# Packing in pieces, moments by tile, and response tables partly on GpSimd, in a Macaron block with 4-bit weights

## The chip, the cores and the metric

The kernel runs on one core of one Trainium2 chip. The metric is the device time of one execution in microseconds. Lower is better. The engines are TensorE (PE; its weight loads are PEld), VectorE (DVE), ScalarE (ACT) and GpSimd (POOL); SyncE (SP) issues nearly all of the transfers.

## The reference

The input is `u`, 2 x 1024 rows of 1024 values, in float32. Three layers with a residual follow each other:

```python
x = u
x = x + 0.5 * ffn(layernorm(x))
x = x + s4(layernorm(x))
x = x + 0.5 * ffn(layernorm(x))

# ffn: 4-bit weights, 8 to a 32-bit word; a scale and a zero point for each group of 128 rows
W = (nibble - (zero + 1)) * scale            # Wg, Wu: 1024 x 2752;  Wd: 2752 x 1024
out = (silu(x @ Wg) * (x @ Wu)) @ Wd

# s4: a causal convolution along the 1024 values of each row
K = s4_kernel(Lambda, p, q, Vc @ Bp, Ct, exp(log_step), 1024)   # needs 1024 complex roots and an inverse DFT
y = irfft(rfft(x, 2048) * rfft(K, 2048))[:1024] + D * x
```

The convolution kernel `K` depends on the parameters alone, and is computed once in the kernel.

## The kernel before

The 2048 rows are four blocks of 512 (`TB`). A block passes twice through the feed-forward layer, which makes eight jobs, in the order of `JOBS`; the convolution of a block lies in the gate/up stage of the job that follows its first pass.

**A job has two stages.** `gate_up` runs over 64 steps: eight waves (`WAVES`) of two or three column tiles of gate and up, and in each wave the eight groups of 128 input rows. The block is held transposed as a high and a low part (`xTh`, `xTl`), so each weight tile is multiplied twice (line 628). The scale of a group is brought in by rescaling: after each group but the last, the accumulator in PSUM is multiplied by the ratio of two groups' scales, on ScalarE for the gate units and on VectorE for most of the up units (`scaled`, lines 598 and 600). After the last group, `gated` makes the product with SiLU (`hf`) and splits it into `hh` and `hl` (lines 655 to 662). `down` runs over 44 steps: two halves of 512 columns, and 22 tiles of the inner dimension in each, with four accumulators that are rescaled in the same way after each of the first 20 tiles. In job 0, ScalarE also takes the second of the four at every other step. `back` turns a finished half and adds it to `x`.

**Weights.** In job 0 the 4-bit words become bytes that are written to device memory (`wq`, `wdq`); every job then loads bytes four steps ahead (`load_bytes`) and converts them three steps ahead to full values (`make_weights`), mostly on GpSimd, in five buffers. Making the bytes has four parts. `fetch` and `fetch_zeros` (for the down matrix `fetch_down`) load words and zero points through SP. `split` and `take_zeros` (`split_down`) run six operations on VectorE: two shifts with masks (lines 453 and 454), and for the even and the odd half an add of the zero points and an xor (lines 461 and 462). `dequantize` (`dequantize_down`) copies each of the eight nibble positions to a byte tile (lines 478 and 510), mostly on GpSimd, and writes it out. The work of wave `w` stands around step `8 * w - 12`, and that of the six row tiles of the down matrix from step 52 of gate/up to step 29 of down.

**Other work.** `moments` and `deviations` compute mean and inverse deviation for 512 rows on VectorE (`BN_STATS` at line 182, then a Newton iteration); `normalized` and `turn` make the transposed block of the next job. In job 1, the tables of the convolution are made by the generator `s4_tables`: poles and weights (`s4_poles`), sums over them by TensorE and the algebra of the roots (`s4_roots`), the response (`s4_response`: `s_k`, line 915) and its Toeplitz blocks `near`, `after`, `ahead`, `middle` (`s4_toeplitz`). Before the change all elementwise work of these but four operations and two fills is on VectorE. One step of the generator is taken in each of 40 steps of gate/up.

**What sets the order.** `fast` hangs functions into dictionaries of hooks by step (`at`), and the stage calls them when it reaches the step. A scheduler then sets the final order of each engine's queue from the dependences. Only what is written through `in_order_of_writing` is held, on the engines named, behind the last instruction of that engine written before it. Two lines show both forms:

```python
at(up, s0 - 1, lambda both=both: in_order_of_writing(both, ET.DVE))   # packing of a wave: held on VectorE
at(up, s, lambda: next(tables, None))                                  # a piece of the tables: not held
```

## Time and profile before

| What | Value |
|---|---|
| median of 3 runs | 2164.68 us (2164.53 to 2165.5) |
| the profiled execution's own time | 2165.84 us |
| its span | 2164.1 us |
| mean granted TensorE clock | 0.993 |
| PE, DVE, ACT, POOL busy | 97%, 80%, 66%, 48% |
| job 0: gate/up, down | 29.1 to 202.8 us, 202.4 to 310.9 us |
| job 1: gate/up, down | 310.9 to 519.8 us, 519.4 to 605.6 us |
| a later job without convolution (7): gate/up, down | 1912.4 to 2069.9 us, 2069.6 to 2151.3 us |

The span is counted from the first to the last instruction; the time holds what lies around it too. The stages in the table are those of the first and last matmuls of their kind. A matmul's record can include some waiting, so a window is judged by its length beside that of the same steps in another job, and the busy time is a hint. A line number is that of the kernel before; in the profile of the changed kernel the same statement has a higher number.

### The profile page before, as it was taken

The numbers are of one execution on the slowest core, as the hardware profiler recorded it, in microseconds if no ns is written. First come the engines' busy times: TensorE is split into PE (matmuls) and PEld (weight loads), VectorE is DVE, ScalarE is ACT, GpSimd is POOL, SyncE is SP. The second block draws the span as 40 slices with busy tenths as digits, with TensorE's granted clock in tenths as the row PEclk, the third lists the DMA queues.
The fourth block names the chain that finished last, engine by engine and source line by source line (L and its number), as shares of the span: only waits on it lengthen the run. The fifth ranks groups of instructions, "written<-read, shape, count | busy, mean of one in ns | idle before, by whom it ended". The sixth has DMA issues, their size and how long they took to land.

```text
span 2164.1 us, 30241 instructions
## 1 busy us (share of the span) xinstructions
PE 2097.0 (97%) x9748; PEld 1429.4 (66%) x9748; DVE 1723.0 (80%) x2831; ACT 1422.9 (66%) x2233; POOL 1038.7 (48%) x1366
## 2 busy tenths in 40 slices
PE   5999899899999999999999999999999999999998
PEld 3555676476867568665776558676686766866576
DVE  7889787778887877778777787878778787777776
ACT  5887677546754677676667767646776467767765
POOL 3868835444345453455335553445534455345642
PEclk9999999999999999999999999999999999999999
DMA  4433321112111311211321121112111121121111
GB/s 141 122 95 116 113 65 42 43 46 80 37 39 51 97 45 46 80 34 33 111 76 42 31 72 35 41 52 74 37 34 40 54 93 44 47 81 36 33 35 57
DMA packets 163543, 132.48 MB, mean 61 GB/s; under 512 B 22252, under 2 KB 151029, under 8 KB 163376
## 3 DMA queue, kind: packets, MB, share of 16 engines
q1 hardware_dynamic: 162528, 129.12, 19.7%
q8 instruction: 79, 1.29, 0.3%
q10 hardware_dynamic: 592, 1.25, 0.2%
q14 instruction: 88, 0.72, 0.1%
q0 software_dynamic: 256, 0.10, 0.0%
HBM read 104.79 MB, written 25.50 MB: 60 GB/s over the span
## 4 chain that ended last, share of the span: by engine, by line
PE 86%; DVE 8%; DMA 2%; POOL 2%; issue 1%; ACT 0%; SPq 0%; DVEq 0%; POOLq 0%; ACTq 0%
PE pg L628 52%; PE po L691 27%; PE pc L993 3%; DVE pg L600 2%; PE pb L713 1%; PE pb L993 1%; DVE po L600 1%; PE pt L219 1%; PE st L219 1%; DVE hf L658 1%; POOL qd L510 1%; DMA raw<-in_L_ffn_up_qweight_dram 0%; PE s_k L915 0%; ACT g L655 0%; DVE hb L674 0%
## 5 line engine op out<-in xcount | busy, mean ns | idle before, releaser
L598 ACT ACTIVATE pg<-pg,rat 128x512 f32<-128x512 f32 x1240 | 786.5, 660 | 435.7 <-PE pg L628 435.0
L600 DVE TENSOR_TENSOR pg<-pg,rat 128x512 f32<-128x512 f32 x1168 | 776.2, 693 | 168.3 <-PE pg L628 163.5
L628 PE MATMUL pg<-xTh,w_up 128*128 128x512 f32 x2752 | 855.1, 438 | 8.3 <-DVE pg L600 6.0
L628 PE MATMUL pg<-xTl,w_up 128*128 128x512 f16 x2752 | 722.8, 383 | 12.4 <-DVE w_up L572 6.6
L576 POOL CAST w_up<-b 128x768 fp32r<-128x768 int8 (+2 forms) x487 | 375.2, 775 | 566.6 <-PE pg L628 454.9
L628 PEld LDWEIGHTS pg<-xTh,w_up 128*128 128x128 f32 x2752 | 519.7, 189 | 185.1 <-DVE pg L600 23.3
L691 PE MATMUL po<-hl,w_down 128*128 128x512 f32 x1344 | 542.7, 406 | 15.5 <-DVE po L600 11.4
L598 ACT ACTIVATE po<-po,ratd 128x512 f32<-128x512 f32 x660 | 431.9, 662 | 167.7 <-PE po L691 167.3
L691 PE MATMUL po<-hh,w_down 128*128 128x512 f32 x1344 | 525.9, 393 | 0.0
L600 DVE TENSOR_TENSOR po<-po,ratd 128x512 f32<-128x512 f32 x620 | 427.1, 697 | 94.1 <-PE po L691 89.9
L628 PEld LDWEIGHTS <-w_up 128*128 128x128 bf16 x2752 | 228.6, 99 | 336.5 <-issue 152.5
L576 POOL CAST w_down<-bd 128x512 fp32r<-128x512 int8 x352 | 222.6, 634 | 417.8 <-PE po L691 357.8
L691 PEld LDWEIGHTS po<-hl,w_down 128*128 128x128 f32 x1344 | 253.9, 189 | 91.9 <-DVE po L600 24.3
L691 PEld LDWEIGHTS po<-hh,w_down 128*128 128x128 f32 x1344 | 254.7, 190 | 45.8
L662 POOL TENSOR_TENSOR hl<-hf,hh 128x512 fp32r<-128x512 f32 x168 | 217.4, 1294 | 8.4
L658 DVE SCALAR_TENSOR_TENSOR hf<-pg,rat,g 128x512 f32<-128x512 f32 x168 | 123.2, 748 | 45.0 <-ACT g L655 39.9
L655 ACT ACTIVATE g<-pg,rat 128x512 f32<-128x512 f32 x168 | 110.8, 687 | 51.2 <-PE pg L628 41.1
L660 POOL CAST hh<-hf 128x512 fp32r<-128x512 f32 x168 | 106.2, 632 | 63.3 <-PE pg L628 37.1
L182 DVE BATCH_NORM_STATS2 stats<-x 128x6 f32<-128x512 f32 x96 | 63.3, 675 | 0.4
L1023 DVE TENSOR_TENSOR x<-x,pc 128x512 f32<-128x512 f32 x32 | 22.0, 686 | 36.4 <-PE pc L993 36.4
L219 PE MATMUL pt<-ident,xn 128*128 128x128 f32 x256 | 43.8, 288 | 7.3 <-ACT xn L1371 7.3
L242 DVE TENSOR_TENSOR xTl<-pt,xTh 128x512 f16<-128x512 f32 x56 | 38.3, 688 | 13.7 <-ACT xTh L241 12.9
(177 smaller groups left out, 1047.8 us busy)
## 6 DMA issues: line engine op xcount, KB each, us to landing
b<-wq SPq DMA_DIRECT2D x319, 96.0 KB
bd<-wdq SPq DMA_DIRECT2D x336, 64.0 KB
x<-in_L_attn_u_dram SPq DMA_DIRECT2D x30, 512.0 KB
b<-wq SPq DMA_DIRECT2D x128, 64.0 KB
xs<-x SPq DMA_DIRECT2D x16, 512.0 KB
x<-xs SPq DMA_DIRECT2D x16, 512.0 KB
out_dram<-x SPq DMA_DIRECT2D x16, 512.0 KB
b<-wq SPq DMA_DIRECT2D x64, 80.0 KB
```

The source lines that it names most:

```text
L182: nc.vector.bn_stats(stats[:, t, i, :], x[b][t][:, bass.ts(i, 512)])
L219: nc.tensor.transpose(ps[:, bass.ts(k, P)], n[:, bass.ts(k, P)], ident)
L576: nc.gpsimd.tensor_copy(t, b)
L598: nc.scalar.activation(dst, src, AF.Copy, scale=sc)
L600: nc.vector.tensor_tensor(dst, src, sc.to_broadcast([P, TB]), ALU.mult)
L628: nc.tensor.matmul(p, weights, (lo, hi)[k][:, g, :], start=(g == 0 and not done), stop=(g == GK - 1 and done), skip_group_check=True,)
L655: nc.scalar.activation(g, pg, AF.Silu, scale=rat[:, 2 * f, GK - 1 :])
L658: nc.vector.scalar_tensor_tensor(hf, pu, last, g, ALU.mult, ALU.mult)
L660: nc.gpsimd.tensor_copy(hi, hf)
L662: nc.gpsimd.tensor_tensor(lo, hf, hi.bitcast(F32), ALU.subtract)
L691: nc.tensor.matmul(ps[c], w[:, bass.ts(c, P)], part, start=(f == 0 and k == 0), stop=(f == NF - 1), skip_group_check=True,)
L993: nc.tensor.matmul(dst, lhsT, rhs, start=start, stop=stop, skip_group_check=True)
```

## The change

Four things are changed, and no arithmetic of the result.

1. `split`, `take_zeros` and `split_down` become one generator, `signed_bytes`, with six pieces. `in_pieces` hangs each piece at a step of its own and holds it in the order of writing on VectorE. The loads for a wave are issued five steps ahead instead of three, those for a row tile of the down matrix seven units ahead instead of three.
2. `moments` becomes a generator by row tile; in job 0 its five pieces lie in steps 3 to 7 of the down stage instead of all in step 0, and what follows from them six steps later than before.
3. The tables of the convolution are cut into 63 pieces over 42 steps, held on VectorE. About half of the elementwise work goes to GpSimd, the large operations in halves of 512 columns.
4. In job 1 the convolution and what follows stand four steps later. In job 0 the block is loaded again at step 27 of the down stage instead of 21, with the turns back at steps 32 to 41; in the other jobs these turns come one step earlier.

The core of the diff:

```diff
     def moments(b, k, then=None):
+        for _ in moments_by_tile(b, k, then):
+            pass
+
+    def moments_by_tile(b, k, then=None):
...
             if then:
                 then(t, mv[:, t, 0:1])
+            yield
...
-    def bytes_of(raw, even):
+    def signed_bytes(key, raw, even, z):
         nc.vector.tensor_scalar(even, raw, 3, NIBBLES, ALU.logical_shift_left, ALU.bitwise_and)
+        yield
         nc.vector.tensor_scalar(raw, raw, 1, NIBBLES, ALU.logical_shift_right, ALU.bitwise_and)
-        return even, raw
-    def signed(part, z):
-        both = part.bitcast(U16)
-        nc.vector.tensor_tensor(both, both, z.bitcast(U16), ALU.add)
-        nc.vector.tensor_scalar(both, both, 0x8080, None, ALU.bitwise_xor)
-        return part.bitcast(I8).rearrange("p (n k) -> p k n", k=4)
+        yield
+        for part in (even, raw):
+            both = part.bitcast(U16)
+            nc.vector.tensor_tensor(both, both, z.bitcast(U16), ALU.add)
+            yield
+            nc.vector.tensor_scalar(both, both, 0x8080, None, ALU.bitwise_xor)
+            yield
+        view = lambda a: a.bitcast(I8).rearrange("p (n k) -> p k n", k=4)
+        packed[key] = view(even), view(raw)
...
+    def in_pieces(at, hooks_and_steps, pieces):
+        held = {}
+        def piece(last):
+            def step():
+                if not held:
+                    held[0] = pieces()
+                for _ in held[0]:
+                    if not last:
+                        break
+            in_order_of_writing(step, ET.DVE)
+        for i, (hooks, s) in enumerate(hooks_and_steps):
+            last = i == len(hooks_and_steps) - 1
+            at(hooks, s, lambda last=last: piece(last))
...
-                at(up, s0 - 3, lambda both=both: in_order_of_writing(both, ET.SP))
-                both = lambda w=w: (split(w), take_zeros(w))
-                at(up, s0 - 1, lambda both=both: in_order_of_writing(both, ET.DVE))
+                at(up, max(0, s0 - 5), lambda both=both: in_order_of_writing(both, ET.SP))
+                steps = [(up, max(1, s0 - d)) for d in (3, 2, 2, 1, 1, 1)]
+                in_pieces(at, steps, lambda w=w: split(w))
...
-                at(*when(max(0, n - 3)), lambda a=a, rt=rt: fetch_down(a, rt))
-                at(*when(max(0, n - 1)), lambda a=a, rt=rt: split_down(a, rt))
+                at(*when(max(0, n - 7)), lambda a=a, rt=rt: fetch_down(a, rt))
+                steps = [when(max(0, n - d)) for d in (4, 3, 3, 2, 1, 0)]
+                in_pieces(at, steps, lambda a=a, rt=rt: split_down(a, rt))
...
-        nc.vector.scalar_tensor_tensor(di, cs, neg[:, 1:2], di, ALU.mult, ALU.add)
+        for own in halves:
+            yield
+            nc.vector.scalar_tensor_tensor(
+                di[:, own], cs[:, own], neg[:, 1:2], di[:, own], ALU.mult, ALU.add
+            )
...
-        nc.vector.tensor_tensor(den, dr, dr, ALU.mult)
...
-        nc.vector.tensor_tensor(sq, di, di, ALU.mult)
-        yield
-        nc.vector.tensor_tensor(den, den, sq, ALU.add)
+        for own in halves:
+            yield
+            nc.gpsimd.tensor_tensor(den[:, own], dr[:, own], dr[:, own], ALU.mult)
+            yield
+            nc.gpsimd.tensor_tensor(sq[:, own], di[:, own], di[:, own], ALU.mult)
+            yield
+            nc.gpsimd.tensor_tensor(den[:, own], den[:, own], sq[:, own], ALU.add)
         for c in range(NC):
             yield
             nc.vector.reciprocal(den[:, bass.ts(c, P)], den[:, bass.ts(c, P)])
...
-        nc.vector.tensor_tensor(poles[0:NST], dr[0:NST], den[0:NST], ALU.mult)
-        yield
-        nc.vector.tensor_tensor(poles[NST:P], di[NST:P], den[NST:P], ALU.mult)
+        for own in halves:
+            yield
+            nc.gpsimd.tensor_tensor(poles[0:NST, own], dr[0:NST, own], den[0:NST, own], ALU.mult)
+            yield
+            nc.gpsimd.tensor_tensor(poles[NST:P, own], di[NST:P, own], den[NST:P, own], ALU.mult)
...
         def op(o, l, r, f):
...
-            nc.vector.tensor_tensor(tmp[o], l, r, f)
+            nc.gpsimd.tensor_tensor(tmp[o], l, r, f)
...
-            nc.vector.tensor_tensor(m0, ec, wide(x0), mul)
-            nc.vector.tensor_tensor(m1, es, wide(x1), mul)
-            nc.vector.tensor_tensor(m0, m0, m1, f)
+            nc.gpsimd.tensor_tensor(m0, ec, wide(x0), mul)
+            nc.gpsimd.tensor_tensor(m1, es, wide(x1), mul)
+            nc.gpsimd.tensor_tensor(m0, m0, m1, f)
+            yield
             nc.vector.tensor_reduce(se[:, i, :], m0, AX.X, add)
...
-        nc.vector.tensor_copy(near[:, 0:3], blocks[:, 0:3])
-        nc.vector.tensor_copy(near[:, 3], blocks[:, 4])
+        yield
+        nc.gpsimd.tensor_copy(near[:, 0:3], blocks[:, 0:3])
+        nc.gpsimd.tensor_copy(near[:, 3], blocks[:, 4])
...
-            nc.vector.tensor_tensor(own, blocks[:, d : d + 5 : 2], blocks[:, 2:7:2], ALU.subtract)
+            nc.gpsimd.tensor_tensor(own, blocks[:, d : d + 5 : 2], blocks[:, 2:7:2], ALU.subtract)
...
+    S4_PIECES = 63
...
-                    late = 30 if j == 1 else 0
+                    late = 34 if j == 1 else 0
...
-                for s in range(2, 42):
-                    at(up, s, lambda: next(tables, None))
+                for i in range(S4_PIECES):
+                    piece = lambda: in_order_of_writing(lambda: next(tables, None), ET.DVE)
+                    at(up, 1 + 42 * i // S4_PIECES, piece)
...
-                    stage, o = (dn, 0) if j == 0 else (up, 44)
-                    at(stage, o, lambda: in_order_of_writing(lambda: moments(ab, 1), ET.DVE))
-                    at(stage, o + 1, lambda: deviations(ab, 1, LIFT))
+                    if j == 0:
+                        steps = [(dn, d) for d in range(3, 8)]
+                        in_pieces(at, steps, lambda: moments_by_tile(ab, 1))
+                        newton = lambda: deviations(ab, 1, LIFT)
+                        at(dn, 8, lambda: in_order_of_writing(newton, ET.DVE))
+                    else:
+                        both = lambda: moments(ab, 1)
+                        at(up, 44, lambda: in_order_of_writing(both, ET.DVE))
+                        at(up, 45, lambda: deviations(ab, 1, LIFT))
...
-                o = 3 if j == 0 else 0
+                o = 9 if j == 0 else 0
...
-            at(dn, 21, lambda: load_x(b, rows_of(u, b) if k == 1 else saved(b)))
+            o, gap = (27, 3) if j == 0 else (21, 4)
+            at(dn, o, lambda: load_x(b, rows_of(u, b) if k == 1 else saved(b)))
             for t in range(NT):
-                at(dn, NF + 5 + 4 * t, lambda t=t: back(b, 0, t))
+                at(dn, o + 5 + gap * t, lambda t=t: back(b, 0, t))
```

## The prediction

> **What bounds the kernel now.** I read the page first, then windows by stage, then who waited for whom in the slow stages, then single groups. TensorE holds the end:
>
> ```profile
> span 2164.1 us, 30241 instructions
> PE 2097.0 (97%) x9748; PEld 1429.4 (66%) x9748; DVE 1723.0 (80%) x2831; ACT 1422.9 (66%) x2233; POOL 1038.7 (48%) x1366
> ...
> PE 86%; DVE 8%; DMA 2%; POOL 2%; issue 1%; ACT 0%; SPq 0%; DVEq 0%; POOLq 0%; ACTq 0%
> ```
>
> The 97% says little of where time can come from, as a stage that waits and one that does not are averaged. The windows view sets each stage of jobs 0 and 1 beside the same stage of a later job, which has the same matmuls and none of the one-time work (columns: window, its length, busy us of PE, PEld, DVE, ACT, POOL, clock, DMA share, GB/s):
>
> ```profile
> 29.10:157.00 127.90, 126.11 (x556) 72.97 (x557) 108.48 (x191) 103.26 (x166) 88.96 (x107) 0.99 0.36 104
> 157.00:202.40 45.40, 42.01 (x177) 22.55 (x176) 42.68 (x66) 33.87 (x56) 38.56 (x53) 1.00 0.52 153
> 202.40:263.00 60.60, 51.39 (x207) 36.72 (x206) 51.88 (x83) 37.32 (x61) 48.16 (x63) 0.92 0.30 93
> 263.00:309.60 46.60, 43.51 (x190) 33.92 (x189) 34.23 (x79) 34.93 (x55) 17.12 (x27) 0.96 0.29 81
> 309.60:519.40 209.80, 200.59 (x982) 129.19 (x980) 164.92 (x302) 121.26 (x194) 93.94 (x118) 0.99 0.15 45
> 519.40:564.40 45.00, 43.98 (x206) 34.89 (x205) 36.20 (x54) 31.84 (x51) 17.78 (x26) 1.00 0.25 79
> 564.40:605.60 41.20, 41.20 (x190) 33.61 (x188) 33.54 (x51) 27.78 (x44) 14.46 (x23) 1.00 0.15 43
> 605.60:793.30 187.70, 187.36 (x929) 122.95 (x929) 153.92 (x272) 112.53 (x178) 92.91 (x118) 1.00 0.19 58
> 2029.40:2069.70 40.30, 40.30 (x179) 23.73 (x177) 29.39 (x44) 28.74 (x45) 20.84 (x30) 1.00 0.14 39
> ```
>
> Row 2 (job 0, gate/up steps 44 to 63) against row 9 (the same steps of job 7): 5.1 us over, DVE 94% busy. Row 3 (job 0, down steps 0 to 21) against row 6: 15.6 over. Row 4 (down steps 22 to 43) against row 7: 5.4 over. Row 5 (job 1, gate/up) against row 8 (job 2): 22.1 over. Row 1 is some 10.5 over job 7's 117.3 us (from the starts of the matmuls of those steps), but 7.2 of that is before 60 us, in the start, whose order hardly changes. From 605 us on there is nothing to win. So this change is worth at most what it takes from about 50 us.
>
> What ends the waits in rows 3 and 4, and TensorE's waits in row 5 (us in total, times, longest):
>
> ```profile
> PE po L691 <- DVE po L600: 8.2, 4, 3.5
> ...
> DVE s_vc L807 <- DMA s_vc<-in_L_attn_Bp_dram: 3.6, 1, 3.6
> ...
> DVE rawd L461 <- DMA zd<-zd_dram: 3.3, 1, 3.3
> PE po L691 <- DVE s_vc L760: 3.1, 1, 3.1
> ```
>
> ```profile
> PE pg L628 <- DVE pg L600: 6.7, 3, 3.8
> PE pb L993 <- POOL sums L988: 1.7, 1, 1.7
> PE s_t L951 <- DMA s_rows<-k_dram: 0.5, 1, 0.5
> ```
>
> It is VectorE each time: a matmul may not go on in a bank until VectorE has scaled it (L600), and the scaling stands behind packing, moments or tables in its queue. Twice VectorE itself stands behind a load.
>
> **The change, part by part.** The sum is made against the profiled execution (span 2164.1, time 2165.84 us); the median of the runs, 2164.68, lies 1.2 below its time, so I subtract the gain from the median.
>
> *Packing in gate/up, job 0.* No instruction goes or comes: two shifts, two adds, two xors for each of eight waves and six row tiles, all still on VectorE. Fetches move two steps earlier on SP's queue, past the writes of the bytes (L482) and the loads of weights (L558) there; the wave's pieces start up to two steps earlier, one to three together between scalings, where the old blocks already had scalings between their parts. The buffers' waits are few, as far as the order shows, so I cost the moved issues at nothing; the cover is the load of weights four steps ahead (about 11 us). If it is gone, GpSimd's conversion is late and TensorE waits about a DMA, 2 us. Row 1: gain 1, ends 0 and 3.
>
> Row 2: before, all three packings of the first column half of down lie here; the order of the changed kernel puts the 88-row one behind `hb`, in the down stage. Price of one:
>
> ```profile
> L461 DVE TENSOR_TENSOR rawd<-rawd,zd 88x1024 uint16<-88x1024 uint16 x2 | 2.2, 1104 | 3.3 <-DMA zd<-zd_dram 3.3
> L462 DVE TENSOR_SCALAR rawd<-rawd 88x1024 uint16<-88x1024 uint16 x2 | 2.3, 1128 | 0.0
> ```
>
> with shifts of 0.65 and 0.79: 5.9 us. DVE falls from 42.7 to 36.8 in a stage that can be 40.3 long, so it is no longer its bound. Bunching still costs about 1.3: 41.8, gain 3.6 (ends 1 and 5).
>
> *Down, first half (row 3).* Here the VectorE sum decides, and it gets more work, not less: 51.9 busy, plus the 88-row packing 5.9, minus the two last pieces of the last packing, which now come after the outputs `y` (1.10 + 1.13 = 2.2), plus one `y` scaling that fell outside the window, 0.7: 56.3 us against TensorE's 45.0. Moments by tile (eight BN_STATS of 0.67, four aggregates of 0.20) cost the same 6 us in five pieces. What goes is the 3.3 us wait for `zd`: its fetch is now seven units ahead instead of three, 3.3 steps or 6 us more. Idle of VectorE remains for ScalarE's gate at the start (1.4) and some for TensorE: 58.5. Gain 2.1; ends 56.3 (gain 4.3) and, if all other idle time stays (8.7 - 3.3), 61.7 (loss 1.1). GpSimd's transposed tiles move from steps 5 to 19 to steps 11 to 25 and meet its `qd` copies (0.77 each); 48 busy of 60 before says it still fits while VectorE holds the pace.
>
> *Down, second half (row 4).* The tables no longer start here, being tied to the order of writing in job 1: the 3.6 us wait for `Bp` goes with the wait it caused. Comes: two turned halves (eight cost 45.0 against 40.6 in job 7, so 1.1 for two) and 2.2 of packing, with half of it hidden. 41.2 + 1.1 + 1.0 = 43.3, gain 3.3 (ends 1 and 5). In later jobs the back transposes come one step earlier; the same instructions, cost nothing, covered by the free banks; 0.2 a job if not.
>
> *Tables (row 5).* 11.7 of the 22.1 is TensorE's own work that stays: 7.5 for `s_k` (L915), 1.7 `s_sums`, 2.5 `s_t`. The rest is stalls, 6.7 of them on VectorE. To GpSimd go 3.6 (L786 to L791), 2.8 (poles), about 1.3 of 128x64 products, the 128x8 operations and 6 of Toeplitz blocks. The row that shows what that is worth, VectorE above and GpSimd below at the same time:
>
> ```profile
> 380.29 1.80 DVE L867 TENSOR_TENSOR s_work<-s_work 128x8 f32<-128x8 f32 x3
> ...
> 382.25 3.91 DVE L867 TENSOR_TENSOR s_work<-s_work 128x8 f32<-128x8 f32 x7
> ```
>
> ```profile
> 382.15 1.28 POOL L662 TENSOR_TENSOR hl<-hf,hh 128x512 fp32r<-128x512 f32 x1
> ```
>
> A 128x8 operation takes 0.17 alone; three of them stretch to 1.2 each while GpSimd works on `hl`, and TensorE's longest wait (3.8, at 386.8) follows. On GpSimd they queue behind `hl` without holding scalings.
>
> The rule that speaks against this is the Trainium skill's GPSIMD Engine Reference, section "Engine selection": elementwise work belongs on VectorE, GpSimd being about twice as slow with two inputs. The trace agrees: 1.29 us for 128x512 on GpSimd (L662), 1.22 for 128x1024 on VectorE (L786). By the rule the table chain gets slower: six squares and sums 7.8, four poles 5.2, 28 small at 0.19 (nearest row: the 128x1 copy, L384), six 128x64 about 0.3, Toeplitz 6, in all about 26 us; were it on the path, that would cost 12 more than VectorE's 14. By the trace GpSimd has 94 of 210 us busy here, and 120 still fits. I take the trace's side for the load, and the rule's for latency: VectorE now waits in order for GpSimd at the first reciprocal, at L875, L878 and both L898. Following the order with these durations, GpSimd is one or two steps early at the reciprocals and within about 1 us of need at the last four. New waits: 0 to 8, I take 1. Moments and convolution four steps later (late 34) end nearer to the next turn: 0.5. Net gain 5 (ends -5 and 9).
>
> Sum: 1 + 3.6 + 2.1 + 3.3 + 5 = 15.0; 2164.7 - 15.0 = 2149.7, and I say 2149.5.
>
> **The rivals.** (A) As summed: half of the stalls go; 13 to 20 us, 2145 to 2152.
>
> (B) VectorE stays the bound. For it: row 3 gets work added. Then row 3 gives -1, row 2 about 2, and GpSimd's latency eats most of row 5 (1 to 2): with 1 and 3, a gain of 6 to 7, 2158.
>
> (C) Spreading ends nearly all stalls: row 3 at 56.3, row 2 at 40.5, row 5 at 9, row 4 at 5, row 1 at 2: 4.3 + 4.9 + 9 + 5 + 2 = 25, 2139. Against: 56.3 is already a VectorE without idle time.
>
> (D) Slower, by one mechanism: the table chain's handovers. VectorE's queue is in order, so a wait at L875, L878 or L898 holds the scalings behind it, and TensorE with them. GpSimd's queue holds `hl` (1.3), `hh` (0.6) and conversions (0.85) that themselves wait for TensorE to free a weight buffer (a step, 2.7). If each of the four comes behind two steps of that, 5.4 each, row 5 loses 21.6 and gains 6: against 10 from the rest that is 2170. It decides from about 4 us at each. Against: conversions run three steps ahead, and GpSimd is idle half the time.
>
> (E) The edits only trade places (the stalls of row 5 come back at GpSimd, row 3 is held by VectorE): within 0.2%, that is 4.3 us, about what a measurement of this kernel tells from no change.
>
> **How the numbers follow.** A 0.55, B 0.22, C 0.13, E 0.06, D 0.04. The range leaves out the far part of C below 2138, E above 2160 and D: 2138 to 2160, about 0.83. Faster by over 0.2%: A, B, C, 0.90; within: 0.06; slower: 0.04.
>
> **What would show it.** In the windows of the changed profile: job 0's steps 44 to 63 near 42 us; its down stage near 102 instead of 107, the first half with VectorE over 95% busy and no wait for `zd`; no `s_vc` work before 300 us; job 1's gate/up near 205 instead of 210, with small TENSOR_TENSOR on POOL and the waits of PE on DVE below 3 us. I am wrong in row 3 if VectorE has idle time there while TensorE waits; wrong in row 5 if DVE waits for POOL `s_work` or `s_cos` by several us; and wrong in kind if anything after 620 us differs by over 2 us.

## The result, and the profile after

The changed kernel takes 2152.4 us in the median of 4 runs (2151.76 to 2153.46), the kernel before 2164.98 in the same comparison (2164.53 to 2165.5). The ratio is 0.9942, with a 95% interval of 0.9925 to 0.996: 12.6 us faster. The profiled execution took 2152.6 us, its span is 2150.7. Its page:

```profile
span 2150.7 us, 30258 instructions
PE 2092.5 (97%) x9748; PEld 1425.5 (66%) x9748; DVE 1704.3 (79%) x2783; ACT 1422.3 (66%) x2233; POOL 1062.5 (49%) x1420
```

These lines hardly differ from those of before. The windows view of the changed kernel, cut at the same steps as the nine rows of the prediction (same columns; rows 7 and 8, 41.3 and 187.7 us long, are left out), tells where the time went:

```profile
29.00:164.40 135.40, 127.33 (x555) 73.84 (x556) 113.77 (x192) 103.75 (x166) 92.62 (x107) 0.97 0.34 98
164.40:209.20 44.80, 42.04 (x178) 22.84 (x176) 37.89 (x59) 34.17 (x56) 32.40 (x44) 1.00 0.55 163
209.20:261.70 52.50, 47.34 (x199) 32.57 (x198) 49.18 (x85) 35.69 (x59) 41.22 (x58) 1.00 0.23 66
261.70:305.40 43.70, 42.67 (x197) 34.09 (x195) 29.91 (x45) 33.59 (x55) 28.43 (x42) 1.00 0.42 129
305.40:505.60 200.20, 199.35 (x982) 128.51 (x981) 150.47 (x287) 123.23 (x197) 115.26 (x172) 0.99 0.16 47
505.60:550.60 45.00, 43.99 (x206) 34.53 (x205) 38.82 (x59) 31.32 (x51) 18.10 (x26) 1.00 0.25 79
...
2016.30:2056.60 40.30, 40.30 (x180) 23.67 (x179) 29.40 (x44) 28.73 (x46) 20.86 (x30) 1.00 0.14 39
```

| Row | before | after | gain | forecast |
|---|---|---|---|---|
| 1: job 0, gate/up steps 0 to 43 | 127.9 | 135.4 | -7.5 | 1 |
| 2: job 0, gate/up steps 44 to 63 | 45.4 | 44.8 | 0.6 | 3.6 |
| 3: job 0, down steps 0 to 21 | 60.6 | 52.5 | 8.1 | 2.1 |
| 4: job 0, down steps 22 to 43 | 46.6 | 43.7 | 2.9 | 3.3 |
| 5: job 1, gate/up | 209.8 | 200.2 | 9.6 | 5 |

The rows sum to 13.7; the spans differ by 13.4, so everything from job 1's down stage on is unchanged within 0.4. The sum came out near the 15.0 forecast, but row 1 has the wrong sign, and rows 3 and 5 make up for it.

**Row 1: two causes that the trace shows.** The first is the start. The timeline of the changed kernel, one engine's instruction to a line (start, length, engine, line; in brackets the idle time before it, and what ended that):

```profile
45.56 0.49 DVE L459 TENSOR_SCALAR even<-raw 128x768 int32<-128x768 int32 x1
...
46.12 0.55 DVE L461 TENSOR_SCALAR raw<-raw 128x768 int32<-128x768 int32 x1
48.09 0.96 DVE L465 TENSOR_TENSOR even<-even,z 128x1536 uint16<-128x1536 uint16 x1 [1.42 <-DMA z<-z_dram]
...
48.96 0.69 DVE L622 TENSOR_TENSOR pg<-pg,rat 128x512 f32<-128x512 f32 x1
...
49.71 0.79 PE L650 MATMUL pg<-xTh,w_up 128*128 128x512 f32 x1 [3.94 <-DVE pg L622]
```

The pieces of wave 2, hung at steps 1 to 3, are held ahead of a scaling. VectorE stands 1.42 us before the add, as the zero points are still under way, and the scaling (L622) that TensorE needs comes behind it: TensorE is idle for 3.94 us, and its matmul then takes 0.79 us, where the two of the same form before the wait took 0.47 and 0.50. In the kernel before, a scaling stood ahead of that add, and the wait was 0.29. The windows view of the same stretch shows the second half of the price, the granted clock (third value from the end):

```profile
46.00:48.00 2.00, 0.00 (x0) 0.00 (x0) 0.67 (x3) 0.00 (x0) 0.00 (x0) 1.00 0.49 159
48.00:50.00 2.00, 0.29 (x1) 0.29 (x1) 1.91 (x3) 0.00 (x0) 1.61 (x2) 0.76 0.17 58
50.00:52.00 2.00, 2.00 (x5) 1.00 (x5) 2.00 (x4) 0.00 (x0) 1.47 (x2) 0.50 0.30 98
52.00:54.00 2.00, 2.00 (x7) 0.67 (x5) 2.00 (x4) 1.73 (x3) 1.47 (x3) 0.50 0.15 49
54.00:56.00 2.00, 2.00 (x6) 1.18 (x5) 0.08 (x1) 1.57 (x4) 2.00 (x3) 0.54 0.68 196
```

By step 8 the kernel is 4.1 us behind that of before. Part of this differs from one execution to another: all traces of kernels with this packing show the wait of 3.8 to 4.2 us, but kernels 4 and 9 of the experiments got 3.4 us of half clock after it instead of 6.8, and their row 1 takes 133.4 and 133.2. The kernel before has 3.4 us of half clock at 47 us as well. Like beside like, some 5.5 of the 7.5 us are the packing's, and some 2 are the longer half clock.

The second cause takes 3.4 us more, in the later waves. The groups of packing operations from 60 to 165 us, before and after (count, total us, mean ns):

```profile
L461 DVE TENSOR_TENSOR even<-even,z 128x1536 uint16<-128x1536 uint16 x2 | 1.9, 946 | 0.0
...
L454 DVE TENSOR_SCALAR raw<-raw 128x768 int32<-128x768 int32 x2 | 1.1, 544 | 0.0
...
L453 DVE TENSOR_SCALAR even<-raw 128x512 int32<-128x512 int32 x2 | 0.8, 422 | 0.0
```

```profile
L465 DVE TENSOR_TENSOR even<-even,z 128x1536 uint16<-128x1536 uint16 x2 | 3.1, 1572 | 0.0
...
L459 DVE TENSOR_SCALAR even<-raw 128x512 int32<-128x512 int32 x2 | 2.3, 1135 | 0.0
L461 DVE TENSOR_SCALAR raw<-raw 128x768 int32<-128x768 int32 x2 | 2.0, 1022 | 0.0
```

The same operation takes up to 2.7 times as long. The timeline of the changed kernel at 70 us shows beside what:

```profile
70.14 1.29 POOL L684 TENSOR_TENSOR hl<-hf,hh 128x512 fp32r<-128x512 f32 x1
70.35 1.50 DVE L461 TENSOR_SCALAR raw<-raw 128x768 int32<-128x768 int32 x1
...
71.37 2.66 POOL L598 CAST w_up<-b 128x768 fp32r<-128x768 int8 x2
...
71.77 1.57 DVE L465 TENSOR_TENSOR even<-even,z 128x1536 uint16<-128x1536 uint16 x1
```

The shift starts 0.2 us after `hl` and ends 0.4 us after `hl` has ended: most of its own 0.55 comes behind GpSimd's instruction. The add does the same behind the conversion. This agrees with the Trainium skill's "SBUF — State Buffer", section "Who interferes with whom": VectorE in a two-port mode and GpSimd share a port pair as an exclusive lock, held by the one that issues first for its whole instruction; with two inputs in SBUF, VectorE contends with a GpSimd instruction that reads SBUF. That the shift runs in such a mode is not shown by any run; its length beside `hl` is. A wave's work stands around step s0 (8w - 12), and its pieces begin at step s0 - 3, which is when GpSimd makes `hh` and `hl` of the wave that has just ended; the old block began at s0 - 1, after it.

**Rows 3 and 4: the clock.** The prediction's own row 3 had a clock of 0.92, and its row 4 one of 0.96; they are 1.00 now. What stood in row 3 of the kernel before, in its timeline:

```profile
228.75 1.48 POOL L239 TENSOR_TENSOR xTl<-turn,xTh 128x512 f16<-128x512 f32 x1
229.00 2.80 DVE L461 TENSOR_TENSOR rawd<-rawd,zd 128x1024 uint16<-128x1024 uint16 x2
230.17 1.08 POOL L238 CAST xTh<-turn 128x512 fp32r<-128x512 f32 x1
...
231.72 2.23 DVE L462 TENSOR_SCALAR rawd<-rawd 128x1024 uint16<-128x1024 uint16 x2
232.23 1.43 POOL L239 TENSOR_TENSOR xTl<-turn,xTh 128x512 f16<-128x512 f32 x1
...
233.87 1.28 DVE L600 TENSOR_TENSOR po<-po,ratd 128x512 f32<-128x512 f32 x2
...
234.61 0.79 PE L691 MATMUL po<-hl,w_down 128*128 128x512 f32 x1 [3.54 <-DVE po L600]
```

and the windows view of that kernel around its two stalls:

```profile
232.00:235.00 3.00, 0.39 (x1) 0.39 (x2) 3.00 (x4) 0.00 (x0) 3.00 (x5) 0.94 0.07 22
235.00:238.00 3.00, 3.00 (x9) 2.31 (x9) 2.94 (x5) 0.85 (x2) 3.00 (x4) 0.50 0.22 66
...
250.00:253.00 3.00, 0.00 (x0) 0.00 (x0) 1.81 (x3) 0.34 (x1) 3.00 (x6) 0.78 0.31 90
253.00:256.00 3.00, 2.98 (x7) 2.41 (x8) 3.00 (x5) 0.68 (x2) 3.00 (x5) 0.50 0.29 84
256.00:259.00 3.00, 3.00 (x11) 2.32 (x11) 1.93 (x2) 1.69 (x3) 3.00 (x5) 0.58 0.73 170
```

A block of packing stands beside GpSimd's work (POOL 3.00 of 3.00), which is in good part the transposed tiles of the next block (`xTl`, `xTh`); they come six steps later now. Stretched so, the block makes TensorE idle for 3.5 us, and then the clock is halved. The clock records of the trace hold two stretches of half clock in row 3, 3.4 and 6.8 us long, and one of 3.4 in row 4: 13.7 us. TensorE was idle for 1.3 us of them anyway, so the other 12.4 cost some 6 us on top of the stalls, by estimate half their length. None is left there after the change.

**Row 5.** TensorE is busy for 199.35 of 200.2 us. In the kernel before, its matmuls waited 6.7 us for scalings, 1.7 for `sums` and 0.5 for `s_rows`. These waits are gone; the longest that is left is 0.6 us, of `s_sums` for `s_vc`. By chance the stage can be 1.7 us shorter still: behind the narrow matmuls of `s_sums` (16 of 128x8) comes half clock for 3.4 us, with no wait over 0.6 us before it. Six of the fourteen traces have it. Those of experiments 7, 10 and 12 do not, and show 198.5 to 198.6 us for this row; that of experiment 8, the same kernel as 7, has it and shows 200.2. VectorE waits for GpSimd nowhere in the stage. The groups of GpSimd's new work there:

```profile
L901 POOL TENSOR_TENSOR s_work<-s_work 128x8 f32<-128x8 f32 x28 | 5.2, 205 | 0.8 <-DVE s_work L911 0.2
...
L822 POOL TENSOR_TENSOR s_cos<-s_cos,s_sq 128x512 f32<-128x512 f32 x2 | 2.5, 1274 | 0.0
```

### The profile page after: what moved, and what is told of

The parts are those of the page before. It is cut to its first block, busy times and chain, and to the rows that moved or that the text cites. A ratio compares the mean times of both kernels' runs of the same rounds, so it can differ in the third digit from the quotient of the medians.

```text
span 2150.7 us, 30258 instructions
## 1 busy us (share of the span) xinstructions
PE 2092.5 (97%) x9748; PEld 1425.5 (66%) x9748; DVE 1704.3 (79%) x2783; ACT 1422.3 (66%) x2233; POOL 1062.5 (49%) x1420
## 4 chain that ended last, share of the span: by engine, by line
PE 87%; DVE 7%; POOL 2%; issue 1%; DMA 1%; ACT 1%; SPq 0%; DVEq 0%; ACTq 0%; POOLq 0%
PE pg L650 53%; PE po L713 27%; PE pc L1040 3%; DVE pg L622 2%; PE pb L735 1%; PE pb L1040 1%; PE pt L224 1%; DVE po L622 1%; PE st L224 1%; POOL w_down L598 0%; DVE hf L680 0%; POOL qd L531 0%; PE s_k L954 0%; DVE even L465 0%; ACT g L677 0%
## 5 line engine op out<-in xcount | busy, mean ns | idle before, releaser
L622 DVE TENSOR_TENSOR pg<-pg,rat 128x512 f32<-128x512 f32 x1168 | 776.1, 693 | 182.4 <-PE pg L650 178.4
L622 DVE TENSOR_TENSOR po<-po,ratd 128x512 f32<-128x512 f32 x620 | 427.0, 697 | 96.6 <-PE po L713 92.6
L713 PEld LDWEIGHTS po<-hl,w_down 128*128 128x128 f32 x1344 | 251.9, 188 | 86.2 <-DVE po L622 20.5
L1040 PEld LDWEIGHTS pc<-near,st 128*128 128x128 f32 x256 | 43.6, 190 | 7.9
```

Source lines behind the costliest of these rows:

```text
L622: nc.vector.tensor_tensor(dst, src, sc.to_broadcast([P, TB]), ALU.mult)
L713: nc.tensor.matmul(ps[c], w[:, bass.ts(c, P)], part, start=(f == 0 and k == 0), stop=(f == NF - 1), skip_group_check=True,)
L1040: nc.tensor.matmul(dst, lhsT, rhs, start=start, stop=stop, skip_group_check=True)
```

## The experiments

Twelve experiments with eleven kernels (7 and 8 have the same one), each compared with the kernel before on the same chip; the medians of before lie between 2164.89 and 2165.75. The changed kernel is the base of all of them, and "kernel 4" is that of experiment 4. What is said of rows and waits comes from one profiled execution of each.

**1. The gate/up packing in its old place.**

```diff
-                at(up, max(0, s0 - 5), lambda both=both: in_order_of_writing(both, ET.SP))
-                steps = [(up, max(1, s0 - d)) for d in (3, 2, 2, 1, 1, 1)]
-                in_pieces(at, steps, lambda w=w: split(w))
+                at(up, s0 - 3, lambda both=both: in_order_of_writing(both, ET.SP))
+                block = lambda w=w: [None for _ in split(w)]
+                at(up, s0 - 1, lambda block=block: in_order_of_writing(block, ET.DVE))
```

> The changed kernel, with the packing of the gate/up waves 2 to 7 back in its old place: loads three steps ahead, one block of six operations at step s0 - 1. The down packing, the moments and the tables stay changed. In the profile of the changed kernel job 0's gate/up ends 6.8 us later than before, 7.5 of it by step 44. Theory 1 (place): the pieces now stand where they hurt, in wave 2 ahead of scalings while their zero points are still under way (TensorE stands 3.9 us at 49.7), in each later wave beside GpSimd's making of hl (a shift takes 1.50 instead of 0.55). Then 6 to 7.5 us come back: about 2145.5. Theory 2 (loads): the earlier loads on SP's queue delay the bytes; then the same time, so this run alone does not part the two. Theory 3: the loss of row 1 is the price of the gain in the down stage, since what is packed earlier is not packed later; then the down stage gets slower by as much and the time stays at 2152.

Measured: 2145.31 us (2143.01 to 2146.09), ratio 0.9911 (0.9898 to 0.9925). Row 1 takes 127.0 us, without half clock in it, and the down stage 96.1 against 96.5. So the loss of row 1 is real, and it buys nothing later: theory 3 falls.

**2. Only wave 2 in its old place.**

```diff
-                at(up, max(0, s0 - 5), lambda both=both: in_order_of_writing(both, ET.SP))
-                in_pieces(at, steps, lambda w=w: split(w))
+                at(up, s0 - 3 if w == 2 else s0 - 5, lambda both=both: in_order_of_writing(both, ET.SP))
+                if w == 2:
+                    ...   # the block of experiment 1
+                else:
+                    in_pieces(at, steps, lambda w=w: split(w))
```

> The changed kernel, with only wave 2 packed as before (loads at step 1, one block at step 3); waves 3 to 7 stay in pieces, with their loads five steps ahead. Theory 1 (place) splits the loss into a start of some 4.1 us, which this gives back, and some 0.5 to 1.5 us in each of five later waves, 3.4 in all, which stay: 2148.3, and the shifts near 70 us still take over 1.2. If the loss is that of the early loads in all waves (theory 2), under 1.5 us come back: 2151.

Measured: 2148.35 us (2146.28 to 2148.62), ratio 0.9923. The first `hf` of the stage starts at 60.5 us instead of 64.0; the add of the even half of waves 3 and 4 still takes 1.57. The start and the later waves are two separate losses of about equal size, as theory 1 has it.

**3. Early loads, pieces two steps later.**

```diff
-                steps = [(up, max(1, s0 - d)) for d in (3, 2, 2, 1, 1, 1)]
+                steps = [(up, max(1, s0 - d)) for d in (1, 1, 1, 0, 0, 0)]
```

> The changed kernel, with the loads still five steps ahead and the packing still in pieces, but at s0 - 1 (three) and s0 (three) instead of s0 - 3 to s0 - 1: after GpSimd has made hl of the wave before. Theory 1 (place): as good as the old place or better, 2145 to 2146.5, no shift over 0.8 us in gate/up steps 8 to 43. Theory 2 (loads): nothing comes back, 2152. A price to look for: the first byte tiles of a wave leave about a step later, so GpSimd may wait for even.

Measured: 2144.89 us (2142.58 to 2145.5), ratio 0.9906. The groups from 60 to 165 us:

```profile
L465 DVE TENSOR_TENSOR even<-even,z 128x1536 uint16<-128x1536 uint16 x2 | 1.9, 943 | 0.0
...
L461 DVE TENSOR_SCALAR raw<-raw 128x768 int32<-128x768 int32 x2 | 1.1, 564 | 0.0
...
L459 DVE TENSOR_SCALAR even<-raw 128x512 int32<-128x512 int32 x2 | 0.8, 420 | 0.0
```

The price of each operation is that of before again, with the loads as early as in the changed kernel, and near 48 us TensorE waits at most 0.8 us at a time. What matters is where a piece stands: in wave 2 behind the arrival of its zero points, in the later waves clear of `hl` on GpSimd. The early loads (theory 2) and the cutting as such cost nothing that can be seen here.

**4 to 6. The tables: hold and GpSimd apart.** In 4 the tables are wholly as before. In 5 they are held in 63 pieces, but their elementwise work is back on VectorE. In 6 only the hold is gone. The core of the three edits, in this order:

```diff
-                for i in range(S4_PIECES):
-                    ...
+                for s in range(2, 42):
+                    at(up, s, lambda: next(tables, None))
...
-            nc.gpsimd.tensor_tensor(tmp[o], l, r, f)
+            nc.vector.tensor_tensor(tmp[o], l, r, f)
...
-                    piece = lambda: in_order_of_writing(lambda: next(tables, None), ET.DVE)
+                    piece = lambda: next(tables, None)
```

> The changed kernel, with the tables of the convolution as before: 40 pieces, not held in the order of writing, all but a few operations on VectorE, late = 30. Packing and moments stay changed. The traces give the tables 9.6 us in job 1's gate/up (209.8 to 200.2) and, if it is their early start that made VectorE wait for Bp in the down stage of job 0, about 3.9 more (steps 33 and 34, 9.0 to 4.0 us): then 2164 to 2166. If the down stage's gain comes from moments and packing alone, it is 2161 to 2162. If the hold and GpSimd were worth what was forecast, 5, it is 2157 to 2158.

> The changed kernel, with the 63 pieces of the tables still held in the order of writing, but all their elementwise work back on VectorE (but the four operations and two fills that GpSimd or ScalarE had before). With the tables as before altogether, the time is 2169.0 (16.6 more than the changed kernel), 8 of it in job 0's down stage and 9 in job 1's gate/up. Theory 1 (order): the hold is what is worth the 16.6, as it keeps the tables out of the down stage and cuts VectorE's bursts; then 2152 to 2154. Theory 2 (GpSimd): what job 1's gate/up gains comes from the 14 us taken off VectorE's queue; then the 9 come back, 2160 to 2162, with TensorE waiting for VectorE 6 us or more there. As forecast, near the middle: 2156.

> The changed kernel, with the same 63 pieces and GpSimd's share of them, but not held in the order of writing on VectorE: the scheduler now puts the s_vc work and the first reciprocals in the second half of job 0's down stage again. Theory 1 (order): the wait for the parameters' loads (Lambda 5.6 and Bp 1.8 us in the kernel with the old tables) is back in the down stage, 5 to 8 us: 2158 to 2160; job 1's gate/up keeps its 200 or gets 203. Theory 2 (GpSimd): what matters is who does the work, and the time stays within 2 us of 2152.4.

| Time; rows 4 and 5, us | not held | held |
|---|---|---|
| on VectorE | 2168.98; 52.2, 209.2 (kernel 4) | 2156.8; 43.7, 205.3 (kernel 5) |
| partly on GpSimd | 2167.2; 53.3, 206.3 (kernel 6) | 2152.4; 43.7, 200.2 (the changed kernel) |

Rows 4 and 5 of kernel 5, then of kernel 6:

```profile
260.70:304.40 43.70, 42.65 (x197) 34.14 (x195) 29.86 (x45) 33.53 (x55) 28.38 (x42) 1.00 0.44 130
304.40:509.70 205.30, 201.37 (x981) 125.95 (x980) 170.63 (x341) 122.86 (x197) 95.05 (x118) 1.00 0.16 45
```

```profile
260.70:314.00 53.30, 46.21 (x197) 35.08 (x195) 37.08 (x83) 35.64 (x57) 34.38 (x47) 0.94 0.36 104
314.00:520.30 206.30, 200.93 (x982) 129.72 (x981) 145.71 (x249) 121.88 (x195) 109.08 (x167) 0.98 0.16 46
```

The ratios to the kernel before are 1.002 (1.0013 to 1.0027), 0.9961 (0.9947 to 0.9974) and 1.0009 (1.0001 to 1.0018). The hold is worth 12 to 15 us. GpSimd's share is worth 4.4 with the hold (the runs of the two kernels do not overlap, though the intervals of the ratios do); the 1.8 without it is not clear of the noise. (Kernel 4 also has the old 40 pieces and `late` = 30.) Kernel 4 is slower than each of its three expectations: the tables' change is worth 16.6 us, more than the whole change brings. With packing and moments changed alone, the kernel is 4 us slower than the one before: with the tables unheld row 4 takes 52.2 us, where the kernel before took 46.6. So the hold mainly keeps the tables out of the room that the other edits make; beside the kernel before, row 4 gains only 2.9. Where it acts, the waits of kernel 6 in the second half of job 0's down stage show:

```profile
PE po L713 <- DVE po L622: 6.1, 3, 5.1
DVE s_vc L801 <- DMA s_vc<-in_L_attn_Lambda_ri_dram: 5.6, 1, 5.6
DVE s_vc L839 <- DMA s_vc<-in_L_attn_Bp_dram: 1.8, 1, 1.8
```

Unheld, the first work on the parameters stands in front of scalings while their loads are under way, and TensorE is idle for 5.1 us and then has 6.8 us of half clock; that half of the down stage takes 53.3 us, and 43.7 with the hold. (The kernel before waited for `Bp` alone, 3.6 us; why `Lambda` is now late as well is not shown.) In job 1 the second price appears, in VectorE's waits in kernel 6:

```profile
DVE s_work L936 <- POOL s_work L934: 4.8, 2, 3.9
...
DVE s_work L915 <- POOL s_work L901: 2.6, 1, 2.6
```

These are the handovers of rival D. They are real where the pieces may bunch: TensorE then stands 3.8 us and gets half clock for 6.8, and the stage takes 206.3 us. With the pieces held apart they vanish. In kernel 5 VectorE has 170.6 us busy in the stage instead of 150.5, and the stage takes 205.3: GpSimd's share is worth about 5 there with the hold, and 2.9 without (209.2 to 206.3). The hold is worth 3.9 in the same stage on VectorE alone, and 6.1 with GpSimd. Of the expectations, theory 1 (order) was right for kernel 6 in direction and too small in size, and "near the middle, 2156" hit kernel 5.

**7 and 8. The down packing as before, twice.**

```diff
-                at(*when(max(0, n - 7)), lambda a=a, rt=rt: fetch_down(a, rt))
-                steps = [when(max(0, n - d)) for d in (4, 3, 3, 2, 1, 0)]
-                in_pieces(at, steps, lambda a=a, rt=rt: split_down(a, rt))
+                at(*when(max(0, n - 3)), lambda a=a, rt=rt: fetch_down(a, rt))
+                block = lambda a=a, rt=rt: [None for _ in split_down(a, rt)]
+                at(*when(max(0, n - 1)), block)
```

> The changed kernel, with the packing of the down matrix as before: loads three units ahead, one block of six operations, not held, one unit ahead. Job 0's down stage took 12.0 us less in the changed kernel, 8.1 of it in the first half, where 2.1 was forecast. Theory 1 (packing): the pieces take adds and xors out of GpSimd's way (an add 0.86 us on average instead of 1.31, an xor 0.50 instead of 1.04) and the earlier load removes the 3.3 us wait for zd; then 6 to 9 us come back: 2158 to 2161. Theory 2 (moments): the gain of the first half is that of the moments' five pieces and the later turns; then 2152 to 2154.

> The kernel with the down packing as before, once more, to see where the long kind of its runs (2157.6 to 2159.2) loses 9 us against the short kind (2149.9). Theory 1 (load): a profile of a long run shows VectorE before L465 or L459 rawd waiting for DMA of zd or rawd, 3 us or more in job 0's last gate/up steps or first down steps, and scalings late behind it. Theory 2 (start): the 9 us lie before 60 us, in the start, where the zero points arrive at different times and TensorE's clock is halved after an idle stretch.

Measured: 2159.01 us (2149.91 to 2159.24, 7 runs), and 2154.56 (2150.02 to 2158.42, 4 runs). The runs lie at 2150 to 2152 or at 2157 to 2159, four of the eleven at the lower. Both profiles are of low runs (2149.91 and 2152.08), with down stages of 92 us. So the size of theory 1 holds for the median of the first only, and its reason is not shown: where the long runs lose their 7 to 9 us stays open, as none was profiled. The mean granted clock, which is measured for every run, tells a part: it is 0.994 or 0.995 in all seven long runs, and 0.996 or 0.997 in all four short ones. By estimate 0.002 of 2155 us is some 4 us, so about half of the loss is half clock; which wait brings it stays open. The profiles do show that job 0's steps 44 to 63 took 45.9 us in one and 49.0 in the other, with VectorE waiting 2.9 and 3.4 us for the words of the first row tile. (The mean xor of row 3 in the changed kernel is 0.59 us, not the 0.50 of the expectation.)

**9. The moments and turns in their old place.**

```diff
-                        steps = [(dn, d) for d in range(3, 8)]
-                        in_pieces(at, steps, lambda: moments_by_tile(ab, 1))
-                        newton = lambda: deviations(ab, 1, LIFT)
-                        at(dn, 8, lambda: in_order_of_writing(newton, ET.DVE))
+                        both = lambda: moments(ab, 1)
+                        at(dn, 0, lambda: in_order_of_writing(both, ET.DVE))
+                        at(dn, 1, lambda: deviations(ab, 1, LIFT))
...
-                o = 9 if j == 0 else 0
+                o = 3 if j == 0 else 0
```

> The changed kernel, with the moments of the next block in one block at step 0 of job 0's down stage again, the turns of it from step 3 on, and all else changed. Theory 1 (packing): 2152 to 2154.5. Theory 2 (moments): the first half of the down stage is slower by 4 to 8 us, with a stall of TensorE behind BN_STATS in steps 1 to 9: 2157 to 2160.

Measured: 2154.65 us (2154.46 to 2157.65), ratio 0.9956. The time lies just above the range of theory 1, but row 3 takes 57.0 us, 4.5 more than in the changed kernel, as theory 2 has it. With kernel 10 this gives row 3 in all four cases, from one profile each. Rows 2 and 3 of kernel 9, then of kernel 10:

```profile
162.90:206.50 43.60, 41.77 (x177) 22.84 (x176) 36.69 (x59) 33.99 (x56) 33.08 (x46) 1.00 0.53 162
206.50:263.50 57.00, 49.70 (x207) 32.84 (x205) 52.27 (x85) 37.66 (x62) 45.10 (x60) 1.00 0.24 71
```

```profile
156.70:205.10 48.40, 43.52 (x177) 22.70 (x176) 45.47 (x70) 34.17 (x56) 39.98 (x54) 0.99 0.53 156
205.10:256.80 51.70, 47.45 (x199) 34.28 (x198) 45.17 (x79) 36.25 (x59) 37.96 (x52) 0.97 0.32 98
```

| Row 3 (rows 2 and 3 together), us | moments as before | moments by tile, later turns |
|---|---|---|
| down packing as before | 60.6 (106.0), the kernel before | 51.7 (100.1), kernel 10 |
| down packing in pieces | 57.0 (100.6), kernel 9 | 52.5 (97.3), the changed kernel |

Row 3 alone would say that moments and turns do everything and the pieces add nothing. But the pieces also push packing from row 2 into row 3, so the two rows belong together. Over both, each edit alone takes out 5 to 6 us, and both take out 8.7. The pieces push work on into row 4 too: over rows 2 to 4 kernel 10 takes 141.9 us and the changed kernel 141.0, so beside the new moments the pieces gain about 1 us, less than profiles of one kernel differ (138.1 and 140.7 in 7 and 8). Whether moments by tile or the later turns do more was not tried apart, nor was the fourth edit by itself. Kernel 10 differs from the kernel before in the tables as well, but those do not reach into row 3: with the tables as before (kernel 4) it is 52.0.

**10. All packing as before; moments and tables changed.** The edits of 1 and 7 together, in short:

```diff
-                in_pieces(at, steps, lambda w=w: split(w))
+                at(up, s0 - 1, lambda block=block: in_order_of_writing(block, ET.DVE))
...
-                in_pieces(at, steps, lambda a=a, rt=rt: split_down(a, rt))
+                at(*when(max(0, n - 1)), block)
```

> The changed kernel with all packing as before, in gate/up and in down: what moments and tables are worth without the packing's change. If the parts add up (7.1 back in gate/up, 6.6 lost in the down stage): 2152, so that the packing's change as a whole is worth nothing; single runs of 2143 to 2145 where the load comes in time. If the down packing needs its early load only because the gate/up packing moved: 2143 to 2146.

Measured: 2144.39 us (2143.71 to 2145.02), ratio 0.9902 (0.9885 to 0.9918). It meets the second expectation's number, though its reason is not shown: without the packing's change the kernel is 8 us faster than with it, and the two intervals lie apart. The first edit of the four cost more than it brought.

**11. Blocks in both, early loads in the down stage.** As kernel 10, but for one line:

```diff
-                at(*when(max(0, n - 3)), lambda a=a, rt=rt: fetch_down(a, rt))
+                at(*when(max(0, n - 7)), lambda a=a, rt=rt: fetch_down(a, rt))
```

> The kernel with the gate/up packing back in its old place (2145.3), with the down packing also in blocks of six at one unit ahead, not held, but its loads still seven units ahead. With blocks and loads three units ahead (and the new gate/up packing) five of seven runs took 2157.6 to 2159.2 and two took 2149.9 and 2151.8; the profiled one was of the short kind, its down stage 92.5 us against the changed kernel's 96.5, its longest wait 2.9 us for the words. Theory 1 (load): the long kind is a block of VectorE standing before a load that comes late; the early load ends that, and a block is no worse than pieces: 2141 to 2143, no spread over 4 us. Theory 2 (pieces): the pieces themselves are worth 6 to 9 us in the down stage: 2150 to 2153.

Measured: 2146.45 us (2145.07 to 2147.44), ratio 0.991. Between the two theories, and no better than kernel 1 (2145.31) or kernel 10: early loads for the blocks bring nothing that can be seen.

**12. The parts put together.**

```diff
+                ahead = 7 if k < 2 else 3
+                at(*when(max(0, n - ahead)), lambda a=a, rt=rt: fetch_down(a, rt))
+                if k < 2:
+                    ...   # in pieces, as in the changed kernel
+                else:
+                    ...   # one block at n - 1, as before
```

> The best parts put together: gate/up packing in its old place; the first two row tiles of the down matrix, which lie in gate/up, in pieces as in the changed kernel; the other four in blocks of six with loads three units ahead, as before; moments and tables changed. In the profiles so far, job 0's gate/up steps 44 to 63 take 44.0 us with pieces and 48.4 with blocks, the second half of its down stage 44.1 with pieces and 42.2 with blocks, and job 1's gate/up 200.2 and 198.5. If the parts add up: 1.5 to 3.5 below the kernel with all packing as before (2144.4): 2141 to 2143. If pieces in gate/up only push work behind the switch of stages, the down stage takes it back: 2144 to 2146.

Measured: 2143.5 us (2142.85 to 2144.84), ratio 0.99 (0.9884 to 0.9917) against a before of 2164.89. Steps 44 to 63 take 44.5 us and job 1's gate/up 198.6, as wished, but the first half of the down stage takes 55.0 against 51.7, as the second expectation describes: the pieces of the first two tiles move work behind the switch of stages. The time lies between the two expectations. It is level with kernel 10, and about 1% faster than the kernel before.

## Why the prediction was right in its number and wrong in its parts

- **Row 1** (forecast 1, was -7.5). The step that failed is "I cost the moved issues at nothing", with "the wave's pieces start up to two steps earlier". In wave 2 the moved pieces wait for the zero points with a scaling behind them. In the later waves a moved piece was priced at its old duration; it stands beside `hl` now and takes up to 2.7 times as long. The row that shows this lock was in the prediction (a 128x8 operation of 0.17 that takes 1.2 beside `hl`), but it was used only for the tables, as a gain. And the forecast set 7.2 us aside as lying "in the start, whose order hardly changes": wave 2 is in the start. Experiments 1 to 3 show both.
- **Row 2** (3.6, was 0.6). VectorE's load was right (37.9 us, forecast 36.8), the length was not: 44.8 against 41.8, with 2.1 us of TensorE's waits for VectorE left. Other kernels with pieces in the down packing took 43.4 to 44.0 here (1, 4, 5, 6 and 9), and kernels with blocks 45.4 to 49.0, so 0.6 is at the low end of what the pieces bring to this row; a part of it comes back in rows 3 and 4.
- **Row 3** (2.1, was 8.1). Two terms. VectorE's sum of 56.3 became 49.2: the packing was carried over at its stretched price, while adds fell from a mean of 1.31 to 0.86 and xors from 1.04 to 0.59, and there are 13 of them: 5.9 us. (In kernel 9 they take 1.08 and 0.62 on average, so the adds' fall comes in good part with the later turns.) And there was no term for the clock, with 0.92 in the row: 10.2 us at half clock, some 4.5 us lost by the estimate above, gone with the stalls ahead of them. The wait for `zd` that the forecast named (3.3) went. Moments costed "the same 6 us in five pieces" hid the rest: with the later turns they are worth 4.5 of this row beside the pieces (kernel 9).
- **Row 4** (3.3, was 2.9). Right: no `s_vc` work before job 1 and no wait for `Bp`. Four packing operations of 4.3 us in all lie here, where two of 2.2 were counted. Part of it is again the clock, 0.96 to 1.00, which the forecast did not count.
- **Row 5** (5, was 9.6). GpSimd's prices were right (0.205 for a small one against 0.19, 1.27 for 128x512 against 1.3), and so was taking the trace's side on load against the rule that GpSimd is slow (the Trainium skill's GPSIMD Engine Reference, "Engine selection"). The 26 us on GpSimd against 14 on VectorE were not like for like, as the 14 leaves out the 28 small operations: from kernel 5 to the changed kernel VectorE's busy time falls by 20.2 us (170.63 to 150.47) and GpSimd's rises by 20.2 (95.05 to 115.26). The mis-sized terms are the share of stalls that go (all, not half) and new waits (none, not 1). The forecast put this row's gain on GpSimd and counted the hold in row 4 only; in kernels 4 to 6 the hold makes 3.9 to 6.1 us of this row, and GpSimd 2.9 to 5.1.
- **Rivals.** C's row 5 came true (9 forecast, 9.6), and D's mechanism exists but only without the hold. The forecast's misses of -8.5, -3.0, 6.0, -0.4 and 4.6 us cancel to -1.3. That the number was right is luck in good part; the account behind it held for row 4 and for the direction of rows 2, 3 and 5.

## What to carry to other kernels

Before moving VectorE work in time, look at what GpSimd does at the new place: price the moved operation by a row beside such an instruction, not by its old row. Sort stalls of TensorE by length, and add the half clock to those of 3 us and more. Where a scheduler may hoist side work, hold it in place before deciding which engine should do it: here the hold was worth 12 to 15 us, and the other engine 2 to 4.

## What the runs showed of the hardware that was not expected

In all fourteen traces, each of the 15 idle stretches of TensorE between 3.1 and 5.1 us in jobs 0 and 1 came with 3.4 or 6.8 us of half clock, which began within the stretch or up to 1.4 us behind it. Of eight stretches of 2.0 to 2.5 us, three were followed by 3.4 us of it. The Trainium skill's "TensorE: Matmul & The Clock Gate", Part 1, gives a reason for the lengths and the chance in them: a free-running window of 3.4 us, of which one idle is enough. The traces agree on 3.4 and its double, but not on the whole. Half clock followed waits of 2.0 and of 3.1 us, which are shorter than such a window. It also came near 48 us in five kernels (before, 2, 3, 10 and 11) after several waits of at most 0.8 us, and in six traces behind the narrow matmuls of `s_sums`, without a long wait. (The records of the clock begin about 32 us into the span and say nothing of what lies ahead.) In jobs 0 and 1 the kernel before has 20.5 us at half clock, the changed kernel 10.2 and kernel 1 only 3.4; up to half of that is time lost. How far the spread of a few us between runs of one kernel comes from it stays open: in kernel 7 the long runs have the lower mean clock, but kernel 12's fastest run has the lowest of its four (0.994 against 0.996 to 0.998).
